# Two attention layers on one core: where in a step the two heads' maxima are turned

## The chip, the core and the metric

The kernel runs on one core of a Trainium2 chip. The metric is device time in microseconds (us) from one launch to its end; a lower number is better. The core's engines are named as in the profile: PE multiplies matrices (PEld is its weight load), DVE is the vector engine, ACT the scalar engine, POOL the third elementwise engine, and SP issues most of the DMAs. Each engine works through its own instructions in program order, and the engines wait for one another through semaphores.

## What is computed

Two layers of self-attention over an image of 64 x 64 positions, batch 2, 256 channels. Layer 0 (normalisation, four heads of 16 channels, a gate and a sigmoid) is not touched by the change. Layer 1 has four heads of 64 channels over 4096 positions:

```python
qkv = jnp.einsum('oc,bchw->bohw', w_qkv, x) + b_qkv[None, :, None, None]
...
attn = jax.nn.softmax(jnp.einsum('bhdn,bhdm->bhnm', q, k) * scale, axis=-1)
out = jnp.einsum('bhnm,bhdm->bhnd', attn, v).reshape(b, c, h, w)
return jnp.einsum('oc,bchw->bohw', w_out, out) + b_out[None, :, None, None] + x
```

All of it is fp32. The softmax needs, for each head and each query, the maximum over the keys, which is subtracted ahead of the exponential.

## The kernel before

Layer 1 is cut into 32 units: a batch element, a pair of heads and a block of 512 queries. A unit goes through 4096 keys in 32 chunks of 128; a chunk is one tile of 128 keys x (2 heads x 512 queries). Keys lie on the partitions, so the maximum over keys is a maximum over partitions. It is taken in two groups of 16 chunks for each unit: DVE keeps a running elementwise maximum `rmax` over the 16 chunks of a group, and at the end of a group PE transposes `rmax`, head by head, in four 128 x 128 pieces into one PSUM bank (`turn_max`, L918), and DVE reduces along the free axis (`fold`, L935). A head's maxima are sent to DRAM, read back as a row for all partitions and put into PSUM as the shift that later chunks are moved by.

The main loop, at the end of the function, goes in steps of two chunks, 16 steps to a unit. Step t handles two chunks afresh, `pair[0]` and `pair[1]`, and, 11 or 12 steps behind, the chunks that got their maxima in the meantime:

- `score` (L888): PE multiplies keys and queries of a chunk into a pair of PSUM banks, of which there are two (`psp`).
- `keep` (L905, L906): DVE takes the chunk into `rmax`, then ACT copies it to a ring of tiles in SBUF. A group's first chunk of a unit (m = 0) has no DVE instruction. A score's banks come free with ACT's copy.
- `shift` (L977) on DVE and `weigh` (L989, exponential on ACT, and L1001, row sums on POOL) of a delayed chunk. In each group one delayed chunk has its shift done by POOL instead (`ALSO`, L966); it falls in the step in which the maxima are turned.
- `gather` (L1030): PE multiplies two delayed chunks with the values.

Each engine's order is the program's order. In a step, PE runs both scores, then the gathers of two chunks, then whatever was hung on the step as "late". DVE runs maximum, shift, maximum, shift. Other work is hung on steps by `at(t, place, step)`, and `hung` runs it at its place; before the change the places of a step are, in order, "start", "early", "early end", "late", "late end" and "end". "start" comes behind both scores and behind the exponential of the odd delayed chunk, "early" directly behind it, "early end" between the two `keep`s, "late" behind the gathers.

Small matrix products (projections of the next keys, values and queries, the sums, the turned maxima and the turned sums) share a single PSUM bank, `misc` (pool `psm`, one buffer). Whoever takes it waits until the user before has been read out.

The maxima are turned in steps 8 and 16 of a unit, once a group of 16 chunks is through. The first head is turned at "early" and folded at "early end"; the second is turned at "late", behind both gathers, and folded at "late end". Step 16 of a unit is also step 0 of the next. In step 8 the bank `misc` still holds a half of the next values (or, in the last eight units, of the output), which ACT copies out at "start" (L844, or L1200).

Of the kernel before, what the change touches and what calls it, by code (L numbers as in the profile page):

```python
# [26 lines left out]
def conv_attention_kernel(  # L27
# [98 lines left out]
    for s in range(3):  # L126
        t = const_prep.tile([P, CC, P], F32, tag=f"wpad{s}", name=f"wpad{s}")
# [27 lines left out]
    for i in range(2):  # L155
        t = const0.tile([P, PB, P], F32, tag=f"negmax0_{i}", name=f"negmax0_{i}")
# [55 lines left out]
    def at(t, place, step):  # L212
        extras.setdefault((t, place), []).append(step)

    def hung(t, place):
        for step in extras.pop((t, place), []):
            step()
# [15 lines left out]
    with own0:  # L233
# [170 lines left out]
        def fold(u):  # L404
            seq(nc.vector.tensor_reduce(
                negmax0[u[1] % 2].rearrange("p i (h e) -> p (i h) e", e=32)[:, :, 0],
                mxs.pop(u), AX.X, ALU.max, negate=True,
            ))
# [147 lines left out]
        for n, u in enumerate(units0):  # L556
            t0 = n * NM
# [5 lines left out]
            if u == units0[-1]:  # L563
                t1 = t0 + NM + 9
# [5 lines left out]
            else:  # L570
                t1 = t0 + NM + 15
# [138 lines left out]
        for i in range(NJ):  # L710
            k = (0, 0, i)
            t1 = T0 + 2 + 2 * i
# [58 lines left out]
    with (  # L771
# [68 lines left out]
        def store_values(b, g, i, half):  # L840
            if half == 0:
                halves_of["v"] = l1.tile([P, NB], F32, tag="kv", name=f"v1s_{b}_{g}_{i}")
            v, cols = halves_of["v"], bass.ts(half, NB // 2)
            seq(nc.scalar.copy(v[:, cols], halves_of.pop("vp")[:, cols]))  # L844
            if half == 1:
                loaded.pop(("kv", b, g, i))
                nc.sync.dma_start(out=vd[b, g, i], in_=v)
# [60 lines left out]
        def turn_max(u, n, k):  # L908

            b, g, j = u  # L910
            if (u, n) == (units[-1], NG - 1):
                if k == 0:
                    late["turns"] = psp.tile([P, 2, NB], F32, tag="pair", name="last_turns")
                ps = late["turns"][:, k, :]
            else:
                ps = misc(f"rt_{b}_{g}_{j}_{n}_{k}")
            for i in range(PB):
                seq(nc.tensor.transpose(  # L918
                    ps[:, bass.ts(i, P)], rmax[u, n][:, k, bass.ts(i, P)], ident
                ))  # L920
            rts[k] = ps
# [273 lines left out]
        def output(b, j, o, part):  # L1195

            if part != 1:
                outs["y"] = l1.tile([P, NB], F32, tag="kv", name=f"y1_{b}_{j}_{o}")
            y, cols = outs["y"], slice(0, NB) if part == 2 else bass.ts(part, NB // 2)
            seq(nc.scalar.activation(  # L1200
                y[:, cols], outs.pop("ps")[:, cols], AF.Identity, bias=bo1[:, o : o + 1]
            ))
            if part == 0:
                return
            xt = loaded["xo", b, j]
            seq(nc.gpsimd.tensor_tensor(xt[:, o, :], xt[:, o, :], y, ALU.add))
            if o == CC - 1:
                nc.sync.dma_start(
                    out=out[b, :, bass.ts(j, NB)].rearrange("(c p) n -> p c n", p=P), in_=xt
                )  # L1210
# [10 lines left out]

        for n, u in enumerate(units):
            b, g, j = u
            t0 = n * US
            if n > 0:
                at(t0 - 9, "start", lambda u=u, b=b, j=j: fetch(("q", u), x1[b][j]))
                for q in range(4):
                    at(t0 - (3, 3, 2, 2)[q], "late", lambda u=u, q=q: next_queries(u, q))  # L1230
                at(t0 - 2, "start", lambda u=u: keep_next_queries(u, 0))
                at(t0 - 1, "start", lambda u=u: keep_next_queries(u, 1))
            if n < len(units) - NJ:
                to = (*units[n + NJ][:2], j)
                at(max(t0 - 1, 0), "start", lambda to=to: fetch(("kv", *to), x1[to[0]][to[2]]))
                for q in range(4):
                    at(t0 + 2 + q, "late", lambda to=to, q=q: next_keys(*to, q))
                    at(t0 + (6, 7, 9, 10)[q], "late", lambda to=to, q=q: next_values(*to, q))
                at(t0 + 6, "start", lambda to=to: store_keys(*to))
                for i, step in enumerate((t0 + 8, t0 + 11)):  # L1240
                    at(step, "start", lambda to=to, i=i: store_values(*to, i))

                t1 = (n // NJ * NJ + NJ - 1) * US
                at(t1 + 2 * j + 2, "start", lambda to=to: load_keys(*to))
                at(t1 + 2 * j + 3 + LAG, "start", lambda to=to: load_values(*to))
            for k in range(NG):
                t1 = t0 + (k + 1) * GS // 2
                places = ("early", "early" if (u, k) == (units[-1], NG - 1) else "late")
                for i, place in enumerate(places):
                    at(t1, place, lambda u=u, k=k, i=i: turn_max(u, k, i))  # L1250
                    at(t1, f"{place} end", lambda u=u, k=k, i=i: fold(u, k, i))
                at(t1 + 2, "end", lambda u=u, k=k: place_shift(u, k))
            t1 = t0 + US + GS // 2
            if u != units[-1]:
                at(t1 + 4, "late", lambda u=u: total(u))
                at(t1 + 5, "start", lambda u=u: keep_total(u))
                at(t1 + 1, "late", lambda u=u: lose(u))
                at(t1 + 7, "late end", lambda u=u: add_sums(u))
                at(t1 + 8, "end", lambda u=u: factors(u))
                for place, k in (("early", 1), ("late", 0)):  # L1260
                    at(t1 + 9, place, lambda u=u, k=k: turn_sums(u, k))
                    at(t1 + 9, f"{place} end", lambda u=u, k=k: rows(u, k))
            else:
                at(END + 1, "late", lambda u=u: last_lost(u))
                at(END + 4, "early", lambda u=u: late_sums((None, None)))
                at(END + 4, "early end", lambda u=u: keep_late(0))
                at(END + 5, "early", lambda u=u: turn_late(0))
                at(END + 5, "early end", lambda u=u: add_late(u, 0))
                at(END + 6, "early", lambda u=u: turn_sums(u, 0))
                at(END + 6, "early end", lambda u=u: first_rows(u))  # L1270
                at(END + LAG, "late", lambda u=u: turn_late(1))
                at(END + LAG, "late", lambda u=u: add_late(u, 1))
                at(END + LAG, "late", lambda u=u: turn_sums(u, 1))
                at(END + LAG, "late", lambda u=u: last_rows(u))
            if n >= len(units) - NJ:
                b0 = B - 2
                at(t0 - 1, "start", lambda b0=b0, j=j: fetch_output(b0, j))
                for o in range(CC):
                    for q in range(4):
                        step = t0 + ((2, 3, 4, 5), (6, 7, 9, 10))[o][q]  # L1280
                        at(step, "late", lambda b0=b0, j=j, o=o, q=q: project_out(b0, j, o, q))
                at(t0 + 6, "start", lambda b0=b0, j=j: output(b0, j, 0, 2))
                for part, step in enumerate((t0 + 8, t0 + 11)):
                    at(step, "start", lambda b0=b0, j=j, part=part: output(b0, j, 1, part))

# [76 lines left out]
        for t in range(max(t for t, _ in extras) + 1):  # L1364
            inside, behind = 0 <= t < END, 0 <= t - LAG < END
            pair = (2 * t, 2 * t + 1)
            scores = [score(c) for c in pair] if inside else []
            if 0 <= t - LAG - 1 < END:
                weigh(pair[1] - 2 * LAG - 2)
            hung(t, "start")  # L1370
            hung(t, "early")
            if inside:
                keep(pair[0], scores[0])
            if behind:
                shift(pair[0] - 2 * LAG)
                weigh(pair[0] - 2 * LAG)
            hung(t, "early end")
            if inside:
                keep(pair[1], scores[1])
            if 0 <= t - LAG - 1 < END:  # L1380
                for c in pair:
                    gather(c - 2 * LAG - 2)
                    if c - 2 * LAG - 2 == 2 * END - 2:
                        keep_late(1)
            hung(t, "late")
            hung(t, "late end")
            if behind:
                shift(pair[1] - 2 * LAG)
            hung(t, "end")
# [67 lines left out]
```

## Time and profile before

| what | us |
|---|---|
| median of 3 runs | 4638.63 (4638.25 to 4638.99) |
| the profiled execution, its own time | 4640.95 |
| its span, first to last instruction | 4639.2 |
| busy in the span: PE / DVE / ACT / POOL | 4499.0 / 3833.4 / 3439.9 / 2514.8 |
| one unit of layer 1 (from 2318.7 us to 2397.6 us) | 78.90 |

Layer 1 begins with its first scores at 2057.8 us, so that its 32 units fill the second half of the span and a little more. A line of the timeline gives the start in us from the span's start, the length in us, the engine, the line, the operation with what it writes and reads, the number of merged instructions, and in brackets the engine's idle time ahead of it and what ended that. One chunk's score is four matmuls in the trace ("x4"), and "x8" is two chunks' worth. DVE instructions overlap a little at their edges: a maximum is listed with 1.22 us, and the next instruction starts 1.13 or 1.14 us after it.

### The profile page before, as it was taken

The page shows a single profiled execution, that of the slowest core. Times are in us where ns is not written, and L with a number is a line of the kernel's source. Part 1 is how long each engine was busy: PE and PEld are TensorE (multiplying, and loading weights), DVE is VectorE, ACT ScalarE, POOL GpSimd, SP SyncE. Part 2 cuts the span into 40 slices and gives each one's busy share as a digit, 9 for nine tenths or more (in the row PEclk, how much of TensorE's full clock was granted, in tenths as well). Part 3 has the DMA queues.
Part 4 walks back from the last instruction along what each step waited for, and adds up shares of the span by engine and source line. Part 5 has one row for each costly group of instructions (what it writes and reads, how often), then busy time and mean ns, then how long its engine had stood idle before and what let it go on. Part 6 is the DMA issues. An engine that isn't in the chain of part 4 may idle for free. (4 is left out here: it accounts for less than half of the span.)

```text
span 4639.2 us, 73122 instructions
## 1 busy us (share of the span) xinstructions
PE 4499.0 (97%) x28490; PEld 1511.6 (33%) x28490; DVE 3833.4 (83%) x4443; ACT 3439.9 (74%) x4588; POOL 2514.8 (54%) x1307
## 2 busy tenths in 40 slices
PE   8999999999999999999999999999999999999998
PEld 3433333333333333333333333333333333323332
DVE  6777777777777777529999999999999999999997
ACT  3266666666666666668888888888888888888885
POOL 5300000000000000008999999999999999999995
PEclk9999999999999999999999999999999999999999
DMA  3100000000000000121111221111211112111213
GB/s 101 39 4 20 20 20 15 15 15 15 15 15 15 15 13 13 33 75 40 35 42 35 55 56 39 37 40 42 71 42 36 39 33 62 51 53 37 53 40 112
DMA packets 190475, 174.84 MB, mean 38 GB/s; under 512 B 120232, under 2 KB 121064, under 8 KB 190128
## 3 DMA queue, kind: packets, MB, share of 16 engines
q1 hardware_dynamic: 188272, 169.58, 13.2%
q8 instruction: 223, 3.65, 0.3%
q14 instruction: 124, 1.02, 0.1%
q10 hardware_dynamic: 1856, 0.59, 0.1%
HBM read 127.65 MB, written 42.48 MB: 37 GB/s over the span
## 5 line engine op out<-in xcount | busy, mean ns | idle before, releaser
L1001 POOL TENSOR_TENSOR acc<-acc,raw 128x1024 f32<-128x1024 f32 x821 | 1950.4, 2376 | 80.1 <-ACT raw L989 30.7
L402 DVE TENSOR_REDUCE mx<-a 128x1 f32<-128x512 f32 x2048 | 1315.5, 686 | 449.9 <-PE a L398 448.8
L439 ACT ACTIVATE p<-s 128x512 f32<-128x512 f32 x2048 | 1108.3, 595 | 702.5 <-PE a L398 367.6
L905 DVE TENSOR_TENSOR rmax<-s,rmax 128x1024 f32<-128x1024 f32 x960 | 1171.6, 1220 | 99.7 <-PE s L888 89.6
L436 PE MATMUL s<-q,kT 32*128 32x512 f32 x4096 | 1218.8, 640 | 0.0
L888 PE MATMUL s<-q,k 64*128 64x512 f32 x4096 | 1120.3, 637 | 98.1 <-ACT raw L906 93.2
L906 ACT COPY raw<-s 128x1024 f32<-128x1024 f32 x1024 | 1035.6, 1011 | 240.8 <-DVE rmax L905 163.5
L977 DVE TENSOR_TENSOR raw<-raw,shift 128x1024 f32<-128x1024 f32 x961 | 1160.7, 1212 | 3.3 <-ACT shift L959 1.8
L989 ACT ACTIVATE raw<-raw 128x1024 f32<-128x1024 f32 x1024 | 1084.9, 1060 | 62.8 <-DVE raw L977 27.7
L398 PE MATMUL a<-kT,q 32*128 32x512 f32 x4096 | 1129.8, 643 | 1.4 <-DVE mx L402 1.3
L1030 PE MATMUL av<-raw,v 128*64 128x512 f32 x4096 | 1007.4, 607 | 4.2 <-ACT raw L989 2.5
L451 PE MATMUL av<-p,v 128*32 128x256 f32 (+1 forms) x7904 | 650.1, 399 | 0.6 <-ACT avs L465 0.6
L501 POOL TENSOR_TENSOR f<-f,dyn 128x16 f32<-128x16 f32 x15 | 3.3, 221 | 1028.2 <-DVE f L500 1028.2
L888 PEld LDWEIGHTS s<-q,k 64*128 64x128 f32 x4096 | 316.8, 185 | 678.7 <-ACT raw L906 487.0
L436 PEld LDWEIGHTS s<-q,kT 32*128 32x128 f32 x4096 | 397.7, 183 | 426.3 <-issue 392.1
L1030 PEld LDWEIGHTS av<-raw,v 128*64 128x64 f32 x4096 | 242.4, 136 | 650.8 <-issue 476.4
L451 PEld LDWEIGHTS av<-p,v 128*32 128x32 f32 x7904 | 157.7, 108 | 751.5 <-issue 737.3
L552 POOL TENSOR_SCALAR res<-res 128x1024 f32<-128x1024 f32 x16 | 16.7, 1044 | 660.3 <-ACT res L551 660.3
L398 PEld LDWEIGHTS a<-kT,q 32*128 32x128 f32 x4096 | 305.2, 184 | 31.4 <-DVE mx L402 18.2
L999 POOL TENSOR_TENSOR acc<-raw,raw 128x1024 f32<-128x1024 f32 x64 | 152.1, 2376 | 60.9 <-ACT raw L989 60.3
L966 POOL TENSOR_TENSOR raw<-raw,row 128x1024 f32<-128x1024 f32 x63 | 151.7, 2407 | 37.9 <-DMA row<-neg 37.9
L935 DVE TENSOR_REDUCE negs<-rt 128x4 f32<-128x512 f32 x126 | 87.0, 690 | 58.8 <-PE rt L918 58.8
(338 smaller groups left out, 1913.5 us busy)
## 6 DMA issues: line engine op xcount, KB each, us to landing
row<-neg SPq DMA_DIRECT2D x64, 512.0 KB
x<-in_x_dram SPq DMA_DIRECT2D x16, 512.0 KB
res<-in_x_dram SPq DMA_DIRECT2D x16, 512.0 KB
x<-res SPq DMA_DIRECT2D x16, 512.0 KB
att<-rows SPq DMA_DIRECT2D x62, 128.0 KB
kd<-k1s SPq DMA_DIRECT2D x24, 256.0 KB
vd<-v1s SPq DMA_DIRECT2D x24, 256.0 KB
k<-kd SPq DMA_DIRECT2D x24, 256.0 KB
```

What stands on the lines that cost most here:

```text
L398: seq(nc.tensor.matmul(ps, qs0[u][r, bass.ts(i, P)], kTs[b][r, bass.ts(m, NB)], start=True, stop=True,))
L402: seq(nc.vector.tensor_reduce(mxs[u][:, i * H + h, m : m + 1], ps, AX.X, ALU.max))
L436: seq(nc.tensor.matmul(ps, kTs[b][r, bass.ts(m, P)], qs0[u][r, :], start=True, stop=True))
L439: seq(nc.scalar.activation(pt[:, k, :], ps, AF.Exp, scale=D0**-0.5))
L451: seq(nc.tensor.matmul(avs[u][32 * h : 32 * h + 32, cols], vs0[b][:, m, 32 * h : 32 * h + 32], pts[t, h // 2][:, h % 2, cols], start=(m == ...
L888: seq(nc.tensor.matmul(ps[:, k, :], ks[b, g, m // PB][r, bass.ts(m % PB, P)], qs1[u][r, :], start=True, stop=True,))
L905: seq(nc.vector.tensor_tensor(rmax[u, n], ps, before, ALU.max))
L906: seq(nc.scalar.copy(raw, ps))
L977: seq(nc.vector.tensor_tensor(raws[t], raws[t], shifts[u, t % NM // GS], ALU.add))
L989: seq(nc.scalar.activation(p, p, AF.Exp, scale=D1**-0.5))
L1001: seq(nc.gpsimd.tensor_tensor(accs[u, n], accs[u, n], p, ALU.add))
L1030: seq(nc.tensor.matmul(avs1[u, n][k * D1 : (k + 1) * D1, :], v[:, m % PB, k, :], raws[t][:, k, :], start=(m % GS == 0), stop=(m % GS == GS ...
```

## The change

The steps that turn maxima get another order, and two new places in a step are made for it: "first", between the two scores and ahead of the odd chunk's exponential, and "between", directly ahead of the second score, behind "start".

```diff
-                for i, step in enumerate((t0 + 8, t0 + 11)):
-                    at(step, "start", lambda to=to, i=i: store_values(*to, i))
+                for i, (step, place) in enumerate(((t0 + 8, "first"), (t0 + 11, "start"))):
+                    at(step, place, lambda to=to, i=i: store_values(*to, i))
...
-                places = ("early", "early" if (u, k) == (units[-1], NG - 1) else "late")
-                for i, place in enumerate(places):
-                    at(t1, place, lambda u=u, k=k, i=i: turn_max(u, k, i))
-                    at(t1, f"{place} end", lambda u=u, k=k, i=i: fold(u, k, i))
+                if (u, k) == (units[-1], NG - 1):
+                    places = ("early", "early end", "early", "early end")
+                else:
+                    places = ("between", "early end", "early end", "late end")
+                for i in range(2):
+                    at(t1, places[2 * i], lambda u=u, k=k, i=i: turn_max(u, k, i))
+                    at(t1, places[2 * i + 1], lambda u=u, k=k, i=i: fold(u, k, i))
...
-                for part, step in enumerate((t0 + 8, t0 + 11)):
-                    at(step, "start", lambda b0=b0, j=j, part=part: output(b0, j, 1, part))
+                for part, (step, place) in enumerate(((t0 + 8, "first"), (t0 + 11, "start"))):
+                    at(step, place, lambda b0=b0, j=j, part=part: output(b0, j, 1, part))
...
-            scores = [score(c) for c in pair] if inside else []
+            scores = [score(pair[0])] if inside else []
+            hung(t, "first")
             if 0 <= t - LAG - 1 < END:
                 weigh(pair[1] - 2 * LAG - 2)
             hung(t, "start")
+            hung(t, "between")
+            if inside:
+                scores.append(score(pair[1]))
             hung(t, "early")
```

In a step that turns maxima PE's order was: score, score, turn of head 0, gather, gather, turn of head 1. It becomes: score, turn of head 0, score, turn of head 1, gather, gather. DVE's order stays as it was: maximum, shift, fold of head 0, maximum, fold of head 1. ACT copies the half of the next values, or of the output, out of `misc` ahead of the odd chunk's exponential and not behind it. No instruction is added or taken away. The last group of the last unit keeps its order.

## The prediction

> **What bounds the kernel now.** I read the page first: in the second half of the span DVE, ACT, POOL and PE all stand at 8 or 9 tenths, so no busy share decides, and the waits of the steps that the change touches must be read. The view of busy time in stretches, for one unit (length, then busy us with counts of PE, PEld, DVE, ACT, POOL):
>
> ```profile
> 2318.70:2397.60 78.90, 75.82 (x362) 24.83 (x362) 73.98 (x69) 69.82 (x76) 74.21 (x37) 1.00 0.15 38
> ```
>
> DVE idles about 4.9 us of 78.9, and POOL about as much. Next come the waits inside layer 1 (2062 to 4570 us): total, times, longest.
>
> ```profile
> DVE rmax L905 <- PE s L888: 89.6, 192, 1.6
> DVE negs L935 <- PE rt L918: 58.8, 94, 1.5
> ```
>
> The second line is what the edit addresses: DVE's folds waiting for turned maxima. The first is what I watch: the running maximum waiting for its score. Third, the timeline of PE and then of DVE over a step 8 (unit 3).
>
> ```profile
> 2315.27 1.13 PE L888 MATMUL s<-q,k 64*128 64x512 f32 x4
> 2316.56 1.13 PE L888 MATMUL s<-q,k 64*128 64x512 f32 x4 [0.16 <-ACT raw L906]
> 2317.94 0.66 PE L918 MATMUL rt<-ident,rmax 128*128 128x128 f32 x4 [0.25 <-ACT v1s L844]
> 2318.53 1.94 PE L1030 MATMUL av<-raw,v 128*64 128x512 f32 x8
> 2320.40 0.66 PE L918 MATMUL rt<-ident,rmax 128*128 128x128 f32 x4
> 2320.99 1.99 PE L888 MATMUL s<-q,k 64*128 64x512 f32 x8
> ```
>
> ```profile
> 2317.59 1.21 DVE L977 TENSOR_TENSOR raw<-raw,shift 128x1024 f32<-128x1024 f32 x1
> 2318.72 0.69 DVE L935 TENSOR_REDUCE negs<-rt 128x4 f32<-128x512 f32 x1
> 2319.32 1.22 DVE L905 TENSOR_TENSOR rmax<-s,rmax 128x1024 f32<-128x1024 f32 x1
> 2321.09 0.69 DVE L935 TENSOR_REDUCE negs<-rt 128x4 f32<-128x512 f32 x1 [0.56 <-PE rt L918]
> 2322.16 1.23 DVE L905 TENSOR_TENSOR rmax<-s,rmax 128x1024 f32<-128x1024 f32 x1 [0.38 <-PE s L888]
> ```
>
> Fold 0 waits for nothing here. Fold 1 waits 0.56 us for its turn, but directly behind it the next step's maximum waits another 0.38 us for its score, which PE starts at 2320.99 after an unbroken row of gathers and turn. So the end of this step is set by PE: fold 1 could be earlier by any amount and the maximum at 2322.16 would not move. Then step 16 (end of unit 3), PE and DVE:
>
> ```profile
> 2354.70 1.13 PE L888 MATMUL s<-q,k 64*128 64x512 f32 x4
> 2356.55 1.13 PE L888 MATMUL s<-q,k 64*128 64x512 f32 x4 [0.72 <-ACT raw L906]
> 2357.61 0.66 PE L918 MATMUL rt<-ident,rmax 128*128 128x128 f32 x4
> ...
> 2360.65 1.99 PE L888 MATMUL s<-q,k 64*128 64x512 f32 x8
> ```
>
> ```profile
> 2355.32 2.34 DVE L977 TENSOR_TENSOR raw<-raw,shift 128x1024 f32<-128x1024 f32 x2
> 2358.30 0.69 DVE L935 TENSOR_REDUCE negs<-rt 128x4 f32<-128x512 f32 x1 [0.65 <-PE rt L918]
> ...
> 2361.83 1.23 DVE L905 TENSOR_TENSOR rmax<-s,rmax 128x1024 f32<-128x1024 f32 x1 [0.27 <-PE s L888]
> ```
>
> Both folds wait (0.65 us, and 0.63 us between these lines), because the unit's first chunk has no maximum and DVE arrives early; yet again the next maximum is released by its score. The same pattern, to some 0.1 us, stands in every unit.
>
> **What the Trainium skill says.** "PSUM — Partial Sum Buffer", section "Engine vs sequencer instructions": matmuls start and complete in program order, and only weight loads can overtake. So whatever turn 1 waits for, the gathers behind it wait too. The trace agrees: at 2317.94 the turn waits 0.25 us for ACT, and the gathers, ready or not, start only 0.59 us after it. The same page, section "PSUM bank collisions raise a hardware error", wants a bank guarded against its readers; the kernel's one `misc` bank then makes turn 1 wait for fold 0's end, which unit 0, which has no gathers yet, shows in pure form:
>
> ```profile
> 2088.31 0.66 PE L918 MATMUL rt<-ident,rmax 128*128 128x128 f32 x4 [0.78 <-DVE negs L935]
> ```
>
> Its fold 0 ran from 2087.56 for 0.69 us, so the turn starts 0.05 to 0.06 us after the fold's end. Third, "TensorE: Matmul & The Clock Gate", section "Part 1: The HAM clock gate", puts the halving of PE's clock at about 3.4 us without work; no run here shows it, and waits of layer 1's scores up to 3.6 us (once) stand beside a granted clock of 1.00.
>
> **The change, part by part.** The count of instructions stays; only PE's order and one ACT copy's place move. What I price is the start of the next step's first score, since it releases DVE in both kinds of step. Spacings from the trace: a score 1.06 us (2356.55 to 2357.61), a turn 0.59 (2317.94 to 2318.53), two gathers 1.87 (2318.53 to 2320.40), score to maximum 1.17 (2320.99 to 2322.16).
>
> Step 8. (a) ACT's copy of `misc` (0.35 us, L844) moves from behind the odd exponential to ahead of it. ACT ends the copy of the chunk before at 2316.51, so this one can end near 2316.9 instead of 2317.9, and turn 0 starts near 2316.95, held by it and not by PE, which is free at 2316.33. (b) The second score follows at 2317.54, 0.98 us later than now; its maximum is due at 2319.32 behind fold 0, and the score is there by 2318.7: hidden, with 0.6 us to spare. (c) The exponential runs up to 0.3 us later; the gathers that need it come later still: hidden. (d) Fold 0 stays at 2318.72, since DVE itself arrives only then. (e) Turn 1, directly behind the second score, would have PE free at 2318.60, but waits for fold 0's end: 2318.72 + 0.69 + 0.05 = 2319.46. That is 0.86 us of idle PE, where now the gathers run. (f) The gathers start at 2319.46 + 0.59 = 2320.05 and the next score at 2320.05 + 1.87 = 2321.92: **0.93 us later** than 2320.99. (g) Fold 1 starts behind its maximum at 2319.32 + 1.14 = 2320.46, its turn being done about then; this saves its wait, but DVE then stands until 2321.92 + 1.17 = 2323.09 for the maximum that now starts at 2322.16. Fold 1's DMAs, issued on SP, leave 0.6 us earlier; the shift that they feed is placed two steps later, and only two waits for that row are on record in all of layer 1 (POOL's first instruction there, and 0.2 us on ACT): nothing gained.
>
> In units 24 to 31 ACT's instruction is the output's (L1200, 0.46 us) and the same sum at 4212.72 gives a score at 4215.92 against 4215.06: 0.86 us. 23 x 0.93 + 8 x 0.86 = 28.3 us. Unit 0 has no gathers, and its second turn and next score are nearer by some 0.6 us (PE waits for ACT and then DVE one after the other there): -0.6 us, once.
>
> Step 16. Turn 0 starts at 2354.70 + 1.06 = 2355.76 and ends its slot at 2356.35, inside the 0.72 us that PE waits anyway for ACT to free a score's banks; the second score stays at 2356.55. Fold 0 no longer waits: two shifts from 2355.32 take 2.26 us, so it runs at 2357.58 instead of 2358.30. Turn 1: 2357.58 + 0.69 + 0.05 = 2358.32, with PE idle from 2357.61. Gathers 2358.91, next score 2360.78 against 2360.65: **0.13 us later**. The wait at the score is merely moved to turn 1. 31 x 0.13 = 4.0 us.
>
> Does a delay stay? Behind step 8 DVE runs without a gap from the late maximum to the end of step 11, and the waits of PE in there are for ACT copies that follow those very maxima, so they move with it; from step 12 to 15 PE has no idle time; behind step 0 DVE goes on almost unbroken to step 8. I find no place that gives it back. POOL and ACT only gain room. Sum: 28.3 - 0.6 + 4.0 = about 32 us. The profiled execution took 4640.95 us (1.7 outside its span of 4639.2), 2.3 above the median; the sum is added to each alike: 4673 for a profiled one, 4638.6 + 32 = 4671 for the median.
>
> Unknown costs, both ends. The semaphore from DVE to a transpose: 0.05 us in unit 0, 0.145 us for the last group's turn behind a maximum (4565.36); I take 0.05, and the other end adds 63 x 0.09 = 6 us. Slack that I have overlooked behind step 8: between nothing and PE's 0.47 us of wait two steps later (2879.07, unit 10); I take nothing, since DVE moves as well; the other end takes off 31 x 0.47 = 15 us. Gathers behind a transpose instead of ahead: the same pair of neighbours, so the same 1.87; +-0.05 us is 3 us.
>
> **The rivals.** A, faster: the folds' waits are the bound and PE catches up. DVE's loss around the two turns (0.56 + 0.38, and 0.65 + 0.63 + 0.27 us) is 2.5 us a unit; if only the part of step 16 were won (0.72 us, its score starting that much earlier) it is 31 x 0.72 = 22 us: 4616. It decides from the point where the next maximum is no longer released by its score. For it: 94 recorded waits. Against: that release stands behind both folds in the records. B, no change: the idle 0.86 us of PE replaces waits further on (0.47 and 0.1 us in steps 10 and 11, 0.2 us a step later), leaving under 9 us: 4643. Against: those waits end with ACT copies of maxima that are late too. C, worse: besides the delay, the two idle stretches slow PE. One 3.4 us window a unit at half clock (the skill's figure, so an estimate) costs 1.7 us x 32 = 54 us: 4725. Against: the stretches are under 1 us each. That the change doesn't do what it says is no rival: the program order is spelled out in it.
>
> **How the numbers follow.** The forecast, 0.79: 4671, by itself 4656 to 4680 from the unknown costs. A 0.09, B 0.06, C and other losses above 0.06. A difference under 0.2% (9 us) can't be told from none by a measurement of this kernel. Slower: 0.79 + 0.06 = 0.85; same 0.06; faster 0.09. The range for 8 in 10 is widened a little at both ends for what I can't see: 4655 to 4685.
>
> **What would show it.** Right: in step 8 turn 1 carries a wait of 0.8 to 0.9 us for "DVE negs", in step 16 one of 0.7 us; the waits of folds for "PE rt" nearly gone; the maximum behind fold 1 waiting about 1.9 us for its score in step 8; a unit 79.9 to 80.0 us. Wrong: units below 78.9, or turn 1 without a wait for fold 0, or the maximum behind fold 1 without one.

## The result, and the profile after

The changed kernel takes 4670.01 us (median of 4 runs, 4669.30 to 4670.56) against 4638.75 us for the kernel before in the same comparison: 1.0068 times as long, 95% interval 1.0053 to 1.0083. The forecast was 4671. The profiled execution took 4669.3 us, its span 4667.5.

One unit in the view of busy time in stretches (unit 3, from its first fold to the next unit's; stretch, length, then busy us and count of PE, PEld, DVE, ACT, POOL):

```profile
2318.70:2398.60 79.90, 75.89 (x360) 24.83 (x360) 73.76 (x69) 69.83 (x76) 74.06 (x37) 1.00 0.15 37
```

On every engine the busy time is that of the unit before within 0.3 us; the unit is 1.00 us longer. The waits inside layer 1 (2062 to 4600 us) of the changed kernel, as total, times, longest:

```profile
DVE rmax L905 <- PE s L888: 175.8, 194, 2.0
DVE negs L935 <- PE rt L918: 0.8, 1, 0.8
DVE rmax L905 <- ACT raw L906: 9.1, 31, 0.3
PE rt L918 <- DVE negs L935: 47.1, 62, 1.1
```

The wait that the edit addresses is gone: 58.8 us of folds waiting for turned maxima have become 0.8. But the running maximum's wait for its score has grown from 89.6 to 175.8 us, and PE has a wait that it didn't have: 62 of the 63 second turns stand for fold 0. Where that sits is seen in the timeline of PE and then of DVE over step 8 of unit 3:

```profile
2315.29 1.13 PE L888 MATMUL s<-q,k 64*128 64x512 f32 x4
2316.86 0.66 PE L918 MATMUL rt<-ident,rmax 128*128 128x128 f32 x4 [0.44 <-ACT v1s L844]
2317.45 1.13 PE L888 MATMUL s<-q,k 64*128 64x512 f32 x4
2319.48 0.66 PE L918 MATMUL rt<-ident,rmax 128*128 128x128 f32 x4 [0.90 <-DVE negs L935]
2320.07 1.94 PE L1030 MATMUL av<-raw,v 128*64 128x512 f32 x8
2321.93 1.99 PE L888 MATMUL s<-q,k 64*128 64x512 f32 x8
```

```profile
2318.74 0.68 DVE L935 TENSOR_REDUCE negs<-rt 128x4 f32<-128x512 f32 x1
2319.34 1.21 DVE L905 TENSOR_TENSOR rmax<-s,rmax 128x1024 f32<-128x1024 f32 x1
2320.47 0.68 DVE L935 TENSOR_REDUCE negs<-rt 128x4 f32<-128x512 f32 x1
2323.11 1.23 DVE L905 TENSOR_TENSOR rmax<-s,rmax 128x1024 f32<-128x1024 f32 x1 [1.96 <-PE s L888]
```

PE stands for 0.90 us at the second turn, and behind it stand two gathers that started at 2318.53 in the kernel before. Fold 1 no longer waits, and DVE spends what it saved, and 1.0 us more, at the next maximum (0.56 and 0.38 us of waits have become one of 1.96). Step 16 of the same unit, PE and DVE:

```profile
2356.70 0.66 PE L918 MATMUL rt<-ident,rmax 128*128 128x128 f32 x4
2357.49 1.13 PE L888 MATMUL s<-q,k 64*128 64x512 f32 x4
2359.25 0.66 PE L918 MATMUL rt<-ident,rmax 128*128 128x128 f32 x4 [0.63 <-DVE negs L935]
...
2361.70 1.99 PE L888 MATMUL s<-q,k 64*128 64x512 f32 x8
```

```profile
2358.51 0.68 DVE L935 TENSOR_REDUCE negs<-rt 128x4 f32<-128x512 f32 x1
2359.49 1.23 DVE L905 TENSOR_TENSOR rmax<-s,raw 128x1024 f32<-128x1024 f32 x1 [0.29 <-ACT raw L906]
2360.63 0.68 DVE L935 TENSOR_REDUCE negs<-rt 128x4 f32<-128x512 f32 x1
...
2362.88 1.23 DVE L905 TENSOR_TENSOR rmax<-s,rmax 128x1024 f32<-128x1024 f32 x1 [1.46 <-PE s L888]
```

The first turn lies in the time in which the second score waited for ACT before, as intended, and the wait comes back at the second turn (0.63 us in place of 0.72). Neither fold waits, and the maximum behind them waits 1.46 us for its score.

### The profile page after: what moved, and what is told of

Read it like the earlier page. It is cut to its first block, busy times and chain, and to the rows that moved or that the text cites. A ratio compares the mean times of both kernels' runs of the same rounds, so it can differ in the third digit from the quotient of the medians.

```text
span 4667.5 us, 73184 instructions
## 1 busy us (share of the span) xinstructions
PE 4497.9 (96%) x28490; PEld 1511.6 (32%) x28490; DVE 3825.9 (82%) x4443; ACT 3439.6 (74%) x4588; POOL 2513.7 (54%) x1307
## 5 line engine op out<-in xcount | busy, mean ns | idle before, releaser
L905 DVE TENSOR_TENSOR rmax<-s,rmax 128x1024 f32<-128x1024 f32 x960 | 1170.7, 1219 | 185.7 <-PE s L888 175.8
L918 PE MATMUL rt<-ident,rmax 128*128 128x128 f32 x504 | 82.6, 286 | 62.7 <-DVE negs L935 47.1
```

The source lines that it names most:

```text
L905: seq(nc.vector.tensor_tensor(rmax[u, n], ps, before, ALU.max))
```

## The experiments

All were compared with runs of the kernel before on the same chip, whose median was 4639.26 us for the first four, 4639.06 for the next four and 4639.64 for the last. In the diffs, the four places are those of turn 0, fold 0, turn 1 and fold 1; k is 0 in step 8 and 1 in step 16.

| kernel | us | ratio to before, 95% interval |
|---|---|---|
| turn1_late | 4631.65 | 0.9984 (0.9977 to 0.9991) |
| only_step8 | 4668.09 | 1.0063 (1.0048 to 1.0078) |
| only_step16 | 4642.11 | 1.0007 (0.9998 to 1.0016) |
| fold_first | 4631.96 | 0.9984 (0.9977 to 0.9991) |
| copy_first | 4628.28 | 0.9978 (0.9969 to 0.9986) |
| mixed | 4623.02 | 0.9966 (0.9953 to 0.9980) |
| turn1_late_less | 4619.44 | 0.9959 (0.9944 to 0.9974) |
| before_less | 4639.36 | 1.0001 (0.9992 to 1.0009) |
| mixed_less | 4609.91 | 0.9937 (0.9920 to 0.9953) |

### The second turn put back behind the gathers

From the changed kernel:

```diff
-                    places = ("between", "early end", "early end", "late end")
+                    places = ("between", "early end", "late", "late end")
```

> As the changed kernel, but the second head's turn stands behind the gathers again (its fold at late end); the first head's turn stays between the scores and the ACT copy stays first. Theory T (the loss is PE standing at the second turn for fold 0 while the gathers queue behind it): the loss goes, and in step 16 the turn between the scores now lies in the wait for ACT, so the next score is 0.58 us earlier than in the kernel before; in step 8 it is 0.07 us later. 4638.7 + 2 - 18 = 4623, or up to 4628 if POOL, which is busy 76.6 of 79 us in the last eight units, takes no gain there. Rival R1 (the turn between the scores delays the second score, and that is the loss) and rival R2 (the ACT copy ahead of the exponential is the loss): both are still in, so about 4670.

Measured 4631.65 us. The loss is gone with this one move, and with the turn between the scores and the moved ACT copy both still in; R1 and R2 fall as the cause of the loss. In step 16 of unit 3 the next score now comes 5.36 us after the step's first one, and 5.95 us before (2354.70 to 2360.65):

```profile
2353.41 1.13 PE L888 MATMUL s<-q,k 64*128 64x512 f32 x4
...
2358.77 1.99 PE L888 MATMUL s<-q,k 64*128 64x512 f32 x8
```

But the time lies 4 us above the upper end of what was expected, which a later experiment takes up.

### Step 8 alone, step 16 alone

From the changed kernel, with step 16 in the order of before:

```diff
-                    places = ("between", "early end", "early end", "late end")
+                    places = (("between", "early end", "early end", "late end"), ("early", "early end", "late", "late end"))[k]
```

> The change in step 8 alone; step 16 has the order of before. T: 0.93 us (0.86 in the last eight units) of each unit's loss stays, 4638.7 + 28 = 4667. If both kinds of step lost alike, about 4654.

The other kernel swaps the two tuples and puts the ACT copy back to "start":

```diff
-                    places = ("between", "early end", "early end", "late end")
+                    places = (("early", "early end", "late", "late end"), ("between", "early end", "early end", "late end"))[k]
...
-                for i, (step, place) in enumerate(((t0 + 8, "first"), (t0 + 11, "start"))):
+                for i, (step, place) in enumerate(((t0 + 8, "start"), (t0 + 11, "start"))):
```

> The change in step 16 alone; step 8 and the ACT copy are as before. T: the wait at the score is only moved to the second turn, 0.13 us a unit, 4638.7 + 4 = 4643. If both kinds of step lost alike, about 4654.

Measured 4668.09 and 4642.11 us: 28.8 and 2.9 us over the kernel before. They add up to 31.7, the whole change's 31.3 within the scatter, and they split as worked out: nearly all of it in step 8. The 2.9 us by itself is not clear of noise (its interval reaches 0.9998).

### The same order on PE, with the fold earlier on DVE

turn1_late takes away a wait and a place in the order at once. This kernel keeps PE's and ACT's order of the changed kernel to the instruction, and lets DVE run fold 0 ahead of the delayed chunk's shift:

```diff
-                    places = ("between", "early end", "early end", "late end")
+                    places = ("between", "fold", "early end", "late end")
...
                 keep(pair[0], scores[0])
+            hung(t, "fold")
             if behind:
                 shift(pair[0] - 2 * LAG)
```

> PE's and ACT's order exactly as in the changed kernel (second turn ahead of the gathers); only DVE's order differs: fold 0 runs ahead of the delayed chunk's shift, so that it ends about 1.1 us earlier. T: the wait of the second turn goes with the fold's lateness, and the next score comes as early as with the turn behind the gathers: 4623 to 4628. Rival R3 (it is the turn's place ahead of the gathers that costs, not its wait), R1 and R2: about 4670.

Measured 4631.96 us, the same as turn1_late within the scatter. The timeline of PE and of DVE, step 8 of unit 3 (which runs here some 1.8 us earlier than in the changed kernel):

```profile
2315.64 1.13 PE L888 MATMUL s<-q,k 64*128 64x512 f32 x4
2316.70 0.66 PE L918 MATMUL rt<-ident,rmax 128*128 128x128 f32 x4
2317.29 1.94 PE L1030 MATMUL av<-raw,v 128*64 128x512 f32 x8
2319.16 2.01 PE L888 MATMUL s<-q,k 64*128 64x512 f32 x8
```

```profile
2315.94 0.68 DVE L935 TENSOR_REDUCE negs<-rt 128x4 f32<-128x512 f32 x1
2316.54 1.21 DVE L977 TENSOR_TENSOR raw<-raw,shift 128x1024 f32<-128x1024 f32 x1
2317.66 1.22 DVE L905 TENSOR_TENSOR rmax<-s,rmax 128x1024 f32<-128x1024 f32 x1
```

Fold 0 ends at 2316.62, ahead of the end of the second score; the second turn follows that score without a wait, and from score to score PE needs 3.52 us where the changed kernel needs 4.48 (2317.45 to 2321.93). The same stretch takes 3.51 us in turn1_late (2316.19 to 2319.70), and no step of a unit differs between the two kernels by more than 0.01 us, so that it isn't a limit elsewhere that makes them equal. So the place of the turn ahead of the gathers costs nothing; the wait at that place costs it all. R3 falls too.

### The ACT copy moved, and nothing else

From the kernel before (with the new place "first" in the loop, and the turns at their old places):

```diff
-                for i, step in enumerate((t0 + 8, t0 + 11)):
-                    at(step, "start", lambda to=to, i=i: store_values(*to, i))
+                for i, (step, place) in enumerate(((t0 + 8, "first"), (t0 + 11, "start"))):
+                    at(step, place, lambda to=to, i=i: store_values(*to, i))
```

(The output's copy is moved in the same way.)

> The kernel before with one edit: in step 8 ACT copies the misc bank out ahead of the odd chunk's exponential; the turns and folds stand as before. Theory T (PE sets the end of step 8): PE's 0.25 to 0.35 us wait of the first turn for that copy goes, the next score comes 0.33 us earlier (2317.62 + 0.59 + 1.87 + 0.59 = 2320.66 against 2320.99), 31 x 0.33 = 10 us: 4629. Rival R2 (the later exponential costs): 4639 or above.

Measured 4628.28 us: this part of the change, by itself, is a gain of 10.8 us where 10 was worked out. PE's timeline in step 8 of unit 3 shows the first turn directly behind the second score:

```profile
2313.12 1.13 PE L888 MATMUL s<-q,k 64*128 64x512 f32 x4
2314.41 1.13 PE L888 MATMUL s<-q,k 64*128 64x512 f32 x4 [0.17 <-ACT raw L906]
2315.47 0.66 PE L918 MATMUL rt<-ident,rmax 128*128 128x128 f32 x4
2316.06 1.94 PE L1030 MATMUL av<-raw,v 128*64 128x512 f32 x8
2317.93 0.66 PE L918 MATMUL rt<-ident,rmax 128*128 128x128 f32 x4
2318.51 2.17 PE L888 MATMUL s<-q,k 64*128 64x512 f32 x8
```

From the step's first score to the next step's it is 5.39 us, against 5.72 before (2315.27 to 2320.99). That 0.33 us went through to the end is also the plainest sign that PE sets this step.

### Where turn1_late left its gain: POOL's load

Here and below, a step's length is taken on DVE, from the start of the step before's second running maximum to that of its own; what PE loses at the end of step 8 thus shows in the length of step 9. In turn1_late steps 0 and 1 were together 0.59 us shorter in each unit than before, as worked out, but step 6 was 0.5 us longer. ACT's timeline there (unit 11), and below it ACT's waits for POOL in layer 1:

```profile
2928.72 1.06 ACT L989 ACTIVATE raw<-raw 128x1024 f32<-128x1024 f32 x1
2930.22 1.01 ACT L906 COPY raw<-s 128x1024 f32<-128x1024 f32 x1 [0.44 <-POOL acc L1001]
2931.13 1.06 ACT L989 ACTIVATE raw<-raw 128x1024 f32<-128x1024 f32 x1
2932.54 1.01 ACT L906 COPY raw<-s 128x1024 f32<-128x1024 f32 x1 [0.36 <-POOL acc L999]
```

```profile
ACT raw L906 <- POOL acc L1001: 21.2, 31, 0.9
ACT raw L906 <- POOL acc L999: 10.6, 30, 0.4
```

The copy takes a tile of the ring that is free once POOL has added the chunk 26 places back. These lines alone prove nothing, since the kernel before has nearly as much of such waits:

```profile
ACT raw L906 <- POOL acc L1001: 23.7, 34, 1.1
```

There 24 of the 34 stand in step 1, and in turn1_late 60 of the 61 stand in steps 4 and 5 (chunks 9 and 10), just ahead of the step that grew. A longer ring wasn't tried; the load on POOL was cut: one row-sum addition a unit (2.4 us) is left out, and the sums lack that chunk.

```diff
-            if on_tensor(t) or m >= NM - 2:
+            if on_tensor(t) or m >= NM - 2 or m == 8:
```

> turn1_late, but POOL leaves out the row-sum addition of one chunk a unit (the 9th of the first group), so that POOL has 2.4 us less in each unit and the sums lack that chunk. Theory P (turn1_late gave back some 10 us because ACT's copy into the ring waits for POOL in steps 5 and 6): the wait goes and the time is 4638.7 + 2 - 18 = 4622 to 4624. If what was given back has another cause, 4631 as turn1_late.

> The control for turn1_late_less: the kernel before, with the same addition left out. P: POOL doesn't set the pace of the kernel before, so 4637 to 4639. If POOL's load sets the pace everywhere, some 8 us or more below 4639.

Measured 4619.44 us with turn1_late and 4639.36 with the kernel before: the same cut brings 12.2 us to the one and nothing to the other. In turn1_late_less POOL's part of ACT's waits shrinks to one line, and step 6 is back at its old length:

```profile
ACT raw L906 <- POOL acc L1001: 1.2, 3, 0.7
```

In before_less ACT's waits for POOL shrink as well, from 24.9 to 2.7 us, and nothing is won by it. So the kernel before has room on POOL for the time that it takes, but not for some 0.6 us a unit less. turn1_late_less lies 3 us below the 4622 to 4624 that were expected; the last experiment shows why.

### A version below both

From the changed kernel:

```diff
-                    places = ("between", "early end", "early end", "late end")
+                    places = (("early", "early end", "late", "late end"), ("between", "early end", "late", "late end"))[k]
```

> Step 8: both scores, then the first turn at early, the second behind the gathers, with the ACT copy first (as in copy_first). Step 16: first turn between the scores, second behind the gathers (as in turn1_late). T: against turn1_late (4631.7) the first turn of step 8 no longer holds the second score behind the ACT copy: 0.07 + 0.33 us a unit, 31 x 0.40 = 12 us: 4619. Rival P2 (POOL has no room left at all): as turn1_late, 4630 to 4632.

Measured 4623.02 us, 0.9966 of the kernel before (0.9953 to 0.9980) and 47 us below the changed kernel: the ACT copy first, the first turn between the scores in step 16 alone, the second turn behind the gathers everywhere. So in step 8 the first turn between the scores does cost something next to the first turn behind them, 8.6 us in all against turn1_late; R1 has that much right. In turn1_late the ACT copy makes up for it. mixed missed its 4619 by 4 us, and the last kernel asked whether that was POOL's doing too:

> mixed with the same addition left out on POOL as in turn1_late_less (one chunk a unit is missing from the row sums). mixed came out 4 us above its 4619. Theory P (the rest is POOL's doing too): with POOL relieved the whole 31 x 0.40 us against turn1_late_less (4619.4) shows: 4607. If step 8 by itself gives less than 0.40 us a unit in this combination: 4610 to 4611.

Measured 4609.91 us: 9.5 us below turn1_late_less and not 12. So POOL is not the cause of the missing 4 us. With POOL relieved, step 9 is 5.06 us in turn1_late_less and 4.79 in mixed_less: 0.27 us a unit, 31 x 0.27 = 8.4 us, which also fits mixed against turn1_late (8.6 us). The term that was wrong is the 0.07 us by which turn1_late was expected to lose in step 8. In before_less step 9 is 5.11 us, so that turn1_late_less wins 0.05 us there, and only 0.33 - 0.05 = 0.28 us are left for mixed_less to add. It fits that ACT's copy ends some 0.1 us earlier than worked out in the changed kernel (first turn at 2316.86 and not 2316.95).

## Why the prediction was right

- **PE sets the end of step 8 (f).** The next score was put at 2321.92 and came at 2321.93; the maximum behind it at 2323.09, and it came at 2323.11. copy_first shows the same from the other side: what PE gets back, the step gets back.
- **Turn 1 waits for fold 0 (e).** Forecast start 2319.46, measured 2319.48, with the wait in its brackets; fold_first takes the wait away without touching PE's order, and the loss goes.
- **The second score behind turn 0 is hidden (b), the exponential too (c).** Score at 2317.45 (forecast 2317.54); its maximum starts without a wait at 2319.34. turn1_late keeps both edits, copy_first the second, and both are faster than the kernel before.
- **Fold 1 wins nothing (g).** It runs at 2320.47 (forecast 2320.46) and the maximum behind it waits 1.96 us (forecast about 1.9).
- **Step 16.** All is 0.93 us later there, by what step 8 lost; with that taken off, fold 0 runs at 2357.58, turn 1 at 2358.32 and the next score at 2360.77, against 2357.58, 2358.32 and 2360.78. Not foreseen was that DVE, with fold 0 early, meets another wait, 0.29 us for ACT's copy of the unit's first chunk (31 times). It lies beside PE's path and costs nothing.
- **A delay stays.** Step 9 is 6.04 us in place of 5.12, steps 0 and 1 together 10.61 in place of 10.50, and no other step differs by over 0.02 us. Rival B falls with this: PE's wait of 0.47 us in step 10, which was to take up the delay, is still 0.47 us (unit 3, at 2326.80 before and 2327.75 after).
- **The sum.** Forecast 32 us; the medians differ by 31.3. By the two kernels with half of the change, step 8 is 28.8 (28.3 less 0.6 forecast) and step 16 is 2.9 (4.0). The two misses of 1.1 us have opposite signs and lie within the scatter; that the sum comes closer than its parts is luck. In the profiled execution, step 9 of unit 0 to step 9 of unit 31 grew by 31.1 us; layer 1 began 1.0 us earlier, the first steps of unit 0 were 1.0 us shorter (0.6 forecast) and the end 0.8 us, so that the span grew by 28.3 us only. All three differ by as much among the other kernels (first running maximum from 2061.8 to 2063.0 us, from there to step 9 of unit 0 from 28.0 to 29.0 us, the end from 103.6 to 104.5 us) and are taken as scatter; the forecast of 0.6 us for unit 0 is thereby neither shown nor refuted.

Rival A had 94 recorded waits for it, and they did go; they were worth nothing because the instruction behind them was released by PE. What would have made it come true is seen in turn1_late: with the second turn behind the gathers, step 16 does win its 0.59 us. Rival C falls: PE stands some 0.90 us (0.80 in the last eight units) and 0.63 us in a unit, and from 2067.1 to 4664.0 us of the changed kernel the granted clock is 1.00.

One reading of the prediction is wrong, though its sum doesn't rest on it: it says that no run here shows PE's clock halved, and that a score's wait of 3.6 us stands beside a clock of 1.00. That wait (3.59 us in the kernel before, at the start of layer 1) ends at 2065.1 us, and from 2066.9 to 2070.1 us the granted clock is 0.50; in the changed kernel a wait of 3.58 us ends at 2064.1 us, and the clock is 0.50 in the stretch around and behind it (the last three numbers of the line are clock, DMA share and GB/s):

```profile
2063.60:2066.90 3.30, 2.79 (x8) 1.13 (x8) 2.63 (x3) 2.48 (x3) 0.00 (x0) 0.50 0.35 132
```

So a stretch of halved clock, some 3.3 us long, is on record next to the one long wait (that the wait is its cause isn't shown), and what speaks against rival C is that beside the waits at the second turn, none over 1.1 us, the clock stays at 1.00.

## What to carry to other kernels

Before a recorded wait is removed, look at the instruction behind it on the same engine: if that one is released by another engine, the wait by itself is worth nothing, and that other engine's row of work is what must get shorter. Where two engines hand one buffer to and fro, the engine that works in order needs other work between the two hand-overs; either fill the gap (gathers ahead of the second turn) or make the answer come sooner (fold 0 ahead of the shift), and here both were worth the same (4631.65 and 4631.96 us). After a gain, the engine with the next least room shows itself: here POOL, through a ring of tiles, took back some three fifths of it (12.2 of 19.6 us).

## What the runs showed of the hardware

A wait of PE for DVE ended sooner behind a reduction than behind an elementwise instruction. PE starts 53 to 56 ns after the recorded end of a reduction (4 waits in the kernel before, 65 in the changed one, 62 of these at the second turn). After that of an elementwise instruction from 8 to 1024 elements wide it starts 145 to 147 ns later (5 waits before, 5 after), so that the width doesn't matter there. One wait of the changed kernel doesn't fit: the first turn of unit 0 starts 90 ns after its running maximum. Why is not known from these runs. For the forecast it meant that the lower end of the two prices (0.05 us) was the right one for the turn behind a fold.
